# Single-row fetches on ScalarE's queue beside SP's, in a graph network's edge loop that gathers with GpSimd

## The chip, the cores and the metric

The kernel runs on one core of a Trainium2 chip. The metric is the device time of one execution in microseconds (us); the time given for a kernel is the median of several runs. A core has TensorE (PE), VectorE (DVE), ScalarE (ACT), GpSimd (POOL) and SyncE (SP). Each has its own instruction queue and works through it in order. DMAs are issued from the queues of SP, ACT and POOL, and 16 DMA engines carry them out.

## What is computed

One layer of a graph network over 12,500 nodes and 200,000 edges, with 64 features for each node and edge, and after it a layer norm. Cut to what matters, with `ssp(v) = softplus(v) - log 2`:

```
nodes    = x[edges]                      # (src, dst) of each edge: 2 x 64 features
gates    = (ssp(edge_state @ We1 + be1) @ We2 + be2) * soft_cutoff(distance)
h        = ssp(nodes @ Wn1 + bn1) @ Wn2 + bn2
sums     = zeros_like(x).at[dst].add(h * gates)
x_new    = x + ssp(sums @ Ws1 + bs1) @ Ws2 + bs2
out      = layernorm(x + x_new)
```

The edges are sorted by `dst`; `src` is random. So the rows `x[src]` have to be gathered one by one, while the `dst` side of 256 neighbouring edges falls into a window of 42 nodes.

## The kernel before

**Groups and steps.** The edges are cut into 391 groups of 512 (`GE`), each in K = 4 slots of 128 edges. A loop (line 573) goes over steps i from -3 to 388; each step does a different stage of several groups, so that the stages of one group are spread over several steps. The order on each engine is the order of the program text (`manual_schedule`). A step before `ends` = 380 does this:

- `load(i + 5)` (line 218): three DMAs on SP, the edge features eT of the group (128 KB) and two tables of 42 rows, wns. Each waits until an earlier group's scatter is over.
- `fetch(i)` (line 203): single rows of x on SP, see below.
- `gather(i + 14)` (line 189): one indirect DMA on POOL for each slot, 128 rows of x by the indices of `src`, into a tile xg; there are 18 such tiles.
- `layer2_edge(i - 1)` (line 282) on PE. Its first matmul (line 285) takes the step's waits in one place: through `behind` it waits for the gather and the one-hot matrix of group i + 3, the copy xT of group i + 1 and the load of group i + 1. The matmuls that need these come later in the step and need not stop for them.
- `layer1_edge(i + 1)` and `layer1_node(i + 1)` (lines 254 and 260) into a PSUM tile z, and the scatter of group i - 3 (line 312), whose result lies in the same tile.
- `exps(i + 1)` and `logs(i + 1)` (lines 271 and 274) on ACT: the exponential and the logarithm of the softplus.
- `transposes(i + 3)` (line 243) on PE, which read the gathered rows, and `xcopy(i + 3)` (line 248) on ACT, which takes them from PSUM to SBUF.
- `layer2_node(i - 1)` (line 295) on PE, and then `hcut`, `message`, `window`, `softplus(i + 1)` and `onehot(i + 5)` on DVE (lines 304, 308, 329, 279 and 234). `window` first loads two register values (line 320).

Whenever enough groups are complete, a block of 512 nodes is finished beside the loop: its parts (25 blocks in all) are put into steps by `BLOCK_STEPS`. From step 380 on the order changes, so that the pipeline runs empty: the transposes come ahead of the matmuls of layer 1, and `layer2(g)` calls `layer2_edge` as before, so that it waits for the gather of group g + 4 (line 287) although its step transposes an earlier group or none. The last group and the last node block follow behind the loop.

**Single rows.** In twelve groups (36, 68, ..., 388, every 32nd: `slots_by_rows`, line 101) POOL gathers only three of the four slots. The 128 rows of the last slot, K - 1, are fetched by SP: in each of the steps 0 to 383, `fetch` loads four indices into SP's registers (line 210) and issues four DMAs of one row of 256 bytes (line 214) into a tile xr, of which there are two. So a slot is complete after 32 steps, and its group is transposed two steps later. For such a group DVE also copies the slot's one-hot columns from xg to xr (line 236). Each of these DMAs is noted among the group's gathers, for which line 285 waits.

Of the kernel before, what the change touches and what calls it, by code (L numbers as in the profile page):

```python
# [42 lines left out]
F32 = mybir.dt.float32  # L43
# [8 lines left out]
SP = mybir.EngineType.SP  # L52
# [4 lines left out]
P = 128  # L57
D = 64
# [3 lines left out]
DW = D + W  # L62
PIECES = 3
NB = 512
K = 4
# [10 lines left out]
ROWS = 4  # L76
# [23 lines left out]

def slots_by_rows(NG):

    return [g for g in range(P // ROWS + 4, NG - 2, P // ROWS)]


@with_exitstack
def gnn_resnorm_kernel(ctx: ExitStack, tc: tile.TileContext, a: dict, out: bass.AP, E: int):
    nc = tc.nc
    x = a["x"]
    N = x.shape[0]  # L110
    NG = a["eT"].shape[1]
# [10 lines left out]
    loads = ctx.enter_context(tc.tile_pool(name="loads", bufs=LOADS + 2))  # L122
# [26 lines left out]
    packed, at = {}, 0  # L149
# [18 lines left out]
    xgs, xrs, eTs = {}, {}, {}  # L168
    made = {}

    def note(key, ins):
        made.setdefault(key, []).append(ins)
        return ins

    def behind(ins, *keys):

        for key in keys:
            for other in made.get(key, []):
                tc.add_manual_dep(ins.ins, other.ins.name,
                                  mybir.DependencyInfo(mybir.DependencyClass.Sync, mybir.DependencyReason.DATA),  # L180
                                  reason="one place of a step takes its waits")

    by_rows = slots_by_rows(NG)
    rows_i = const.tile([len(by_rows), P], I32, name="rows_i")

    def padding(g, k):
        return g * GE + k % 2 * HE + k // 2 * P >= E

    def gather(g, after=False):

        xg = loads.tile([P, K, P], F32, name="xg", bufs=AHEAD + BEHIND)
        xgs[g] = xg
        if after:
            nc.vector.memset(xg[:, 0, :1], 0.0)
        for k in range(K - (g in by_rows)):
            if padding(g, k):
                nc.vector.memset(xg[:, k, :D], 0.0)
                continue
            note(("gather", g), nc.gpsimd.indirect_dma_start(  # L199
                out=xg[:, k, :D], out_offset=None, in_=x,  # L200
                in_offset=bass.IndirectOffsetOnAxis(ap=src_i[:, g, k : k + 1], axis=0)))

    def fetch(i):

        n, r = divmod(i * ROWS, P)
        if i < 0 or n >= len(by_rows):
            return
        if r == 0:
            xrs[by_rows[n]] = loads.tile([P, P], F32, name="xr", bufs=2)
        _, at = nc.values_load_multi_w_load_instructions(  # L210
            rows_i[n : n + 1, r : r + ROWS], engines=[SP], min_val=0, max_val=N - 1,
            skip_runtime_bounds_check_because="src holds rows of x")
        for j, v in enumerate(at):
            note(("gather", by_rows[n]), nc.sync.dma_start(xrs[by_rows[n]][r + j : r + j + 1, :D], x[bass.ds(v, 1), :]))  # L214

    bases = {}

    def load(g):
# [13 lines left out]

    def onehot(g):
        last = nc.vector.tensor_tensor(xgs[g][:, :, D:DW], iota, rel[:, g, :].to_broadcast([P, K, W]), OP.is_equal)  # L234
        if g in by_rows:
            last = nc.vector.tensor_copy(xrs[g][:, D:DW], xgs[g][:, K - 1, D:DW])
        note(("onehot", g), last)

    def transposes(g):
        tx = tx_tile()[:DW].rearrange("f (k e) -> f k e", k=K)  # L240
        for k in range(K):
            row = xrs[g][:, :DW] if g in by_rows and k == K - 1 else xgs[g][:, k, :DW]
            nc.tensor.transpose(tx[:, k, :], row, ident)  # L243
        xTs[g] = tx

# [33 lines left out]
        nc.vector.scalar_tensor_tensor(ss[g].rearrange("p i t e -> p (i t e)")[:, part], us[g][:, part], BIG,  # L279
                                       z_of(g)[:, part], OP.min, OP.max)  # L280

    def layer2_edge(g):
        gh = gh_tile()
        v = gh.rearrange("p (i t h d) -> p i t h d", i=2, t=2, h=2)
        first = nc.tensor.matmul(gh, ones3[:, :P], row3.rearrange("q i k d -> q (i k d)"), start=True, stop=False,  # L285
                                 skip_group_check=True)
        behind(first, ("gather", g + 4), ("onehot", g + 4), ("xcopy", g + 2), ("load", g + 2))
        for t in range(2):
            nc.tensor.matmul(v[:, 0, t], ss[g][:, 0, t, :], we2, start=False, stop=False, skip_group_check=True)  # L289
        ghs[g] = gh.rearrange("p (i k d) -> p i k d", i=2, k=K)  # L290
# [128 lines left out]
    with tc.manual_schedule():  # L419
# [4 lines left out]
        with tc.tile_pool(name="prep", bufs=1) as prep:  # L424
# [67 lines left out]
            for i, w in enumerate((we2[:D, 0, :], wn2)):  # L492
                n = w.shape[0]
# [16 lines left out]
            rows = prep.tile([PIECES, 4, D], BF16, name="rows")  # L510
# [6 lines left out]
            for i in range(PARTS):  # L517
# [19 lines left out]
                if i == 2:  # L537
# [5 lines left out]
                    for t in range(2):  # L543
                        r = rel[:, :, 2 * t : 2 * t + 2]
# [3 lines left out]
        with tc.tile_pool(name="finish", bufs=1) as finish:  # L548
            blocks = list(zip(node_blocks(N), block_steps(N, NG)))
            last = NG - 1  # L550
            ends = last - CATCH_UP
            second, third, ahead = {}, {}, {}
# [12 lines left out]
            def at(f, g, *more):  # L565
                if 0 <= g < NG:
                    f(g, *more)
# [5 lines left out]
            for i in range(-3, last - 1):  # L573
                now = parts.pop(i, [])
                early = [part for part in now if part.tensor]
                at(load, i + LOADS)
                fetch(i)
                if i >= 0:
                    at(gather, i + AHEAD, i < BEHIND)
                if i < ends:  # L580
                    for g in second[i]:
                        layer2_edge(g)
                    if i >= -1:
                        zs[i + 1] = z_tile()
                        layer1_edge(i + 1)
                        for part in early:
                            part.tensor(tx_tile())
                    if i >= -1:
                        layer1_node(i + 1)
                    for n, g in enumerate(third[i]):  # L590
                        scatter(g, zs[i + 1][:, 1, HE + 2 * W * n : HE + 2 * W * (n + 1)])
                    at(exps, i + 1)
                    at(logs, i + 1)
                    for g in ahead[i]:
                        transposes(g)
                        xcopy(g)
                    for g in second[i]:
                        layer2_node(g)
                    for g in second[i]:
                        hcut(g)  # L600
                        message(g)
                    for g in third[i]:
                        window(g)
                    for part in early:
                        part.others()
                    at(softplus, i + 1)
                else:
                    for g in ahead[i]:
# [73 lines left out]
            for part in begun:  # L682
# [4 lines left out]
                         skip_runtime_bounds_check_because="a comparison's result")  # L687
    with tc.If(far > 0), tc.tile_pool(name="outside", bufs=1) as o:
# [7 lines left out]
        with tc.For_i(0, NG, 1) as g:  # L696
# [38 lines left out]
            v = gh.rearrange("p (i k d) -> p i k d", i=2, k=K)  # L735
# [27 lines left out]
def layouts(inputs):  # L763
# [3 lines left out]
    x = np.asarray(inputs["x"])  # L767
# [3 lines left out]
    N, E = x.shape[0], src.shape[0]  # L771
# [10 lines left out]

    out = {"x": np.ascontiguousarray(x)}
    out["src_l"] = lanes(src, 0)
    out["rows"] = np.ascontiguousarray(out["src_l"].reshape(P, NG, K)[:, slots_by_rows(NG), K - 1].T)
    out["dst_l"] = lanes(dst, dst[-1])
    out["dist_l"] = lanes(dist, 1e6)
    out["dst_h"] = np.ascontiguousarray(padded(dst, NR * P * HE, dst[-1]).reshape(NR, P, HE).transpose(1, 0, 2))
# [42 lines left out]
```

## Time and profile before

| | |
|---|---|
| time, median of 3 runs | 2012.66 us (2009.44 to 2016.36) |
| profiled execution: its own time | 2006.9 us |
| profiled execution: span, first to last instruction | 2005.1 us |
| mean granted TensorE clock | 0.971 of full speed |
| PE busy | 1853.3 us, 92% |
| POOL busy | 1477.0 us, 74%, 1555 instructions |
| DVE busy | 1079.6 us, 54% |
| ACT busy | 921.0 us, 46% |
| row DMAs on SP (line 214) | 1536, 228 ns each on the queue (median) |

In the profile, L199 means line 199 of the kernel. An entry of a group ends with the busy time in us, the mean duration in ns, the idle time of the engine just ahead of these instructions, and after an arrow what ended most of that idle time. PEld is TensorE's weight load, which lies beside its matmuls; SPq is SP's queue, where issuing a DMA isn't counted as busy. Where an instruction waits for several things, the profile names the one that came last by its own account; if the one named had long been over, it was another. The granted clock is 1.00 when TensorE runs at its full clock.

### The profile page before, as it was taken

How to read it: one execution, taken by the hardware profiler on the slowest of the kernel's cores; microseconds unless marked ns; L12 is line 12 of the kernel's file. 1: busy time of each engine (PE TensorE's matmuls, PEld its weight loads, DVE VectorE, ACT ScalarE, POOL GpSimd, SP SyncE). 2: the span in 40 equal slices, each digit the busy share in tenths (PEclk: the TensorE clock that was granted, in tenths of full speed). 3: DMA queues.
4: the chain of work that ended last, by engine and by line, in shares of the span. 5: the costliest groups of instructions: out<-in, count | busy, mean ns of one | idle time of the engine just before them, and what ended most of it. 6: DMA issues, size and time to landing. Idle time of an engine off the chain costs nothing.

```text
span 2005.1 us, 41203 instructions
## 1 busy us (share of the span) xinstructions
PE 1853.3 (92%) x11373; PEld 1539.3 (77%) x11373; DVE 1079.6 (54%) x2744; ACT 921.0 (46%) x1318; POOL 1477.0 (74%) x1555
## 2 busy tenths in 40 slices
PE   5899999989999988998999899999999999999997
PEld 4788888877777777777777777778777777777875
DVE  4455555544554554545555555545555555555654
ACT  1355555544444444444444444445444444444543
POOL 6777777777777777777777777777777777777770
PEclk9999999999999999999999999989999999998997
DMA  8422222222222222222222222222222222222320
GB/s 238 131 69 70 70 71 69 71 65 62 66 65 65 62 65 65 65 65 67 62 68 65 65 68 64 68 61 71 70 66 68 67 68 68 68 70 64 74 63 12
DMA packets 170980, 143.09 MB, mean 71 GB/s; under 512 B 46475, under 2 KB 142915, under 8 KB 170746
## 3 DMA queue, kind: packets, MB, share of 16 engines
q1 hardware_dynamic: 119746, 87.95, 15.1%
q0 software_dynamic: 49632, 50.92, 13.4%
q10 hardware_dynamic: 1368, 1.51, 0.3%
q8 instruction: 97, 1.59, 0.3%
q14 instruction: 137, 1.12, 0.2%
HBM read 130.57 MB, written 9.63 MB: 70 GB/s over the span
## 4 chain that ended last, share of the span: by engine, by line
PE 81%; DMA 6%; ACT 5%; issue 3%; DVE 2%; SPq 2%; POOL 0%; DVEq 0%; ACTq 0%
PE z L260 17%; PE gh L289 12%; PE z L254 12%; PE gh L295 12%; PE z L312 8%; PE gh L285 6%; PE tx L243 6%; PE z L252 4%; DMA eT<-in_eT 4%; ACT u L271 2%; ACT u L274 2%; PE z L522 2%; PE tx L348 1%; PE tx L379 1%; SPq L214 1%
## 5 line engine op out<-in xcount | busy, mean ns | idle before, releaser
L199 POOL DMA_INDIRECT xg<-in_x,src_i x1551 | 1476.8, 952 | 480.4 <-issue 343.9
L271 ACT ACTIVATE u<-z 128x768 f32<-128x768 f32 x392 | 317.4, 810 | 981.4 <-PE z L312 953.6
L304 DVE TENSOR_TENSOR h<-gh,cut 128x256 f32<-128x256 f32 x391 | 166.0, 425 | 707.7 <-PE gh L295 702.7
L260 PE MATMUL z<-xT,wns 106*128 106x256 f32 x1564 | 422.2, 393 | 0.0
L295 PE MATMUL gh<-consts,s 128*128 128x64 f32 x3128 | 396.4, 270 | 0.0
L295 PEld LDWEIGHTS gh<-consts,s 128*128 128x128 f32 x3128 | 384.9, 194 | 0.0
L279 DVE SCALAR_TENSOR_TENSOR s<-u,z 128x768 f32<-128x768 f32 x392 | 372.7, 951 | 20.0 <-ACT u L274 6.8
L274 ACT ACTIVATE u<-u,one 128x768 f32<-128x768 f32 x392 | 365.8, 933 | 12.7
L260 PEld LDWEIGHTS z<-xT,wns 106*128 106x128 f32 x1564 | 306.8, 198 | 46.6 <-ACT xT L248 0.7
L289 PE MATMUL gh<-consts,s 128*128 128x128 f32 x1564 | 281.0, 302 | 0.0
L254 PE MATMUL z<-eT,consts 128*128 128x256 f32 x782 | 280.3, 441 | 0.0
L289 PEld LDWEIGHTS gh<-consts,s 128*128 128x128 f32 x1564 | 205.8, 191 | 91.5 <-issue 91.0
L312 PEld LDWEIGHTS z<-xg,msg 128*128 128x128 f32 x1512 | 237.4, 198 | 22.5
L285 PE MATMUL gh<-row,ones 3*128 3x512 bf16 x391 | 148.7, 380 | 105.6 <-DMA eT<-in_eT 28.2
L243 PE MATMUL tx<-consts,xg 128*106 128x128 f32 x1552 | 239.6, 278 | 4.1 <-DVE xg L234 2.7
L248 ACT COPY xT<-tx 106x512 f32<-106x512 f32 x391 | 221.4, 566 | 15.8 <-PE tx L243 15.8
L312 PE MATMUL z<-xg,msg 128*128 128x84 f32 x1512 | 223.5, 271 | 0.0
L329 DVE TENSOR_TENSOR sums<-sums,z 64x42 f32 x756 | 148.6, 197 | 131.2 <-ACT xT L248 108.1
L243 PEld LDWEIGHTS tx<-consts,xg 128*106 128x106 f32 x1552 | 185.3, 144 | 5.0 <-DVE xg L234 3.0
L308 DVE TENSOR_TENSOR msg<-gh,h 128x256 f32<-128x256 f32 x391 | 165.8, 424 | 13.4
L254 PEld LDWEIGHTS z<-eT,consts 128*128 128x128 f32 x782 | 118.4, 191 | 47.9 <-issue 2.2
L285 PEld LDWEIGHTS <-ones 3*128 3x128 bf16 x391 | 35.4, 91 | 142.3 <-ACT u L274 58.1
(101 smaller groups left out, 682.6 us busy)
## 6 DMA issues: line engine op xcount, KB each, us to landing
eT<-in_eT SPq DMA_DIRECT2D x391, 128.0 KB
xg<-in_x,src_i POOLq DMA_INDIRECT x1551
xr<-in_x SPq DMA_DIRECT2D x1536, 0.2 KB
wns<-table SPq DMA_DIRECT2D x782, 21.0 KB
table<-tb SPq DMA_DIRECT2D x14, 448.0 KB
sums<-in_xT SPq DMA_DIRECT2D x7, 455.0 KB
y<-in_x SPq DMA_DIRECT2D x24, 128.0 KB
out<-y SPq DMA_DIRECT2D x24, 128.0 KB
```

The lines of the kernel that those rows point to most:

```text
L199: note(("gather", g), nc.gpsimd.indirect_dma_start(out=xg[:, k, :D], out_offset=None, in_=x, in_offset=bass.IndirectOffsetOnAxis(ap=src_i[ ...
L243: nc.tensor.transpose(tx[:, k, :], row, ident)
L248: note(("xcopy", g), nc.scalar.copy(xT, xTs[g]))
L254: nc.tensor.matmul(zs[g][:, 0, :HE], we1.rearrange("a h d -> a (h d)"), eTs[g], start=False, stop=True, skip_group_check=True)
L260: nc.tensor.matmul(zn, wns[:, g % REST, h, :], xTs[g][:, h], start=True, stop=True, skip_group_check=True)
L271: nc.scalar.activation(us[g][:, part], z_of(g)[:, part], AF.Exp)
L274: nc.scalar.activation(us[g][:, part], us[g][:, part], AF.Ln, bias=one)
L279: nc.vector.scalar_tensor_tensor(ss[g].rearrange("p i t e -> p (i t e)")[:, part], us[g][:, part], BIG, z_of(g)[:, part], OP.min, OP.max)
L285: first = nc.tensor.matmul(gh, ones3[:, :P], row3.rearrange("q i k d -> q (i k d)"), start=True, stop=False, skip_group_check=True)
L289: nc.tensor.matmul(v[:, 0, t], ss[g][:, 0, t, :], we2, start=False, stop=False, skip_group_check=True)
L295: nc.tensor.matmul(ghs[g][:, 1, 2 * t + h, :], ss[g][:, 1 + h, t, :], wn2, start=False, stop=h == 1 and t == 1, skip_group_check=True)
L312: ins = nc.tensor.matmul(sc, msgs[g][:, 2 * t : 2 * t + 2, :].rearrange("p h f -> p (h f)"), xgs[g][:, 2 * t : 2 * t + 2, D:DW], start=t = ...
```

## The change

The number of slots fetched by single rows is doubled. In each of the twelve groups slot K - 2 is now fetched in this way too, so that POOL gathers two of the four slots there. SP goes on fetching slot K - 1. ACT's queue fetches slot K - 2: in each step one load of four indices into ACT's registers and two row DMAs stand between the exponential and the logarithm, and two more between the logarithm and the copy xT. The new tiles have a name for each of the two slots, two buffers each. The calls on ACT stand in the branch for steps before 380; the rows of steps 380 to 383, the last 16 of slot K - 2 of group 388, are therefore not fetched, and ACT issues 380 x 4 = 1520 of them.

The second part concerns the waits of line 285. In steps before 380 they are put together from the groups which the step itself transposes (`ahead[i]`, which is i + 3 there), and are the same as before. From step 380 on `layer2_edge` is called without any, so that each instruction waits for its own inputs alone.

```
 def slots_by_rows(NG):
-    return [g for g in range(P // ROWS + 4, NG - 2, P // ROWS)]
+    return [(g, k) for k in (K - 1, K - 2) for g in range(P // ROWS + 4, NG - 2, P // ROWS)]
...
+    half_of = {nc.sync: 0, nc.scalar: len(by_rows) // 2}
...
-        for k in range(K - (g in by_rows)):
+        for k in range(K):
+            if (g, k) in by_rows:
+                continue
...
-    def fetch(i):
+    def fetch(i, engine, first=0, count=ROWS):
-        n, r = divmod(i * ROWS, P)
-        if i < 0 or n >= len(by_rows):
+        n, r = divmod(i * ROWS + first, P)
+        if i < 0 or n >= len(by_rows) // 2:
             return
+        n += half_of[engine]
         if r == 0:
-            xrs[by_rows[n]] = loads.tile([P, P], F32, name="xr", bufs=2)
-        _, at = nc.values_load_multi_w_load_instructions(
-            rows_i[n : n + 1, r : r + ROWS], engines=[SP], min_val=0, max_val=N - 1,
-            skip_runtime_bounds_check_because="src holds rows of x")
-        for j, v in enumerate(at):
-            note(("gather", by_rows[n]), nc.sync.dma_start(xrs[by_rows[n]][r + j : r + j + 1, :D], x[bass.ds(v, 1), :]))
+            xrs[by_rows[n]] = loads.tile([P, P], F32, name=f"xr{by_rows[n][1]}", bufs=2)
+        if first == 0:
+            _, row_at[engine] = nc.values_load_multi_w_load_instructions(
+                rows_i[n : n + 1, r : r + ROWS], engines=[engine.engine], min_val=0, max_val=N - 1,
+                skip_runtime_bounds_check_because="src holds rows of x")
+        for j in range(count):
+            note(("gather", by_rows[n][0]), engine.dma_start(xrs[by_rows[n]][r + j : r + j + 1, :D],
+                                                             x[bass.ds(row_at[engine][first + j], 1), :]))
...
     def onehot(g):
...
-        if g in by_rows:
-            last = nc.vector.tensor_copy(xrs[g][:, D:DW], xgs[g][:, K - 1, D:DW])
+        for k in range(K):
+            if (g, k) in by_rows:
+                last = nc.vector.tensor_copy(xrs[g, k][:, D:DW], xgs[g][:, k, D:DW])
...
-    def layer2_edge(g):
+    def layer2_edge(g, *needs):
...
-        behind(first, ("gather", g + 4), ("onehot", g + 4), ("xcopy", g + 2), ("load", g + 2))
+        behind(first, *needs)
...
-                fetch(i)
+                fetch(i, nc.sync)
...
                 if i < ends:
+                    needs = [("xcopy", i + 1), ("load", i + 1)]
+                    needs += [(name, g) for g in ahead[i] for name in ("gather", "onehot")]
                     for g in second[i]:
-                        layer2_edge(g)
+                        layer2_edge(g, *needs)
...
                     at(exps, i + 1)
+                    fetch(i, nc.scalar, 0, ROWS // 2)
                     at(logs, i + 1)
+                    fetch(i, nc.scalar, ROWS // 2, ROWS // 2)
                     for g in ahead[i]:
                         transposes(g)
                         xcopy(g)
```

More of the change, by code (lines that the diff above doesn't have):

```diff
@@ L201, in gather @@
                 in_offset=bass.IndirectOffsetOnAxis(ap=src_i[:, g, k : k + 1], axis=0)))
-    def fetch(i):
-        n, r = divmod(i * ROWS, P)
-        if i < 0 or n >= len(by_rows):
+    def fetch(i, engine, first=0, count=ROWS):
+        n, r = divmod(i * ROWS + first, P)
+        if i < 0 or n >= len(by_rows) // 2:
             return
+        n += half_of[engine]
         if r == 0:
-            xrs[by_rows[n]] = loads.tile([P, P], F32, name="xr", bufs=2)
-        _, at = nc.values_load_multi_w_load_instructions(
-            rows_i[n : n + 1, r : r + ROWS], engines=[SP], min_val=0, max_val=N - 1,
-            skip_runtime_bounds_check_because="src holds rows of x")
-        for j, v in enumerate(at):
-            note(("gather", by_rows[n]), nc.sync.dma_start(xrs[by_rows[n]][r + j : r + j + 1, :D], x[bass.ds(v, 1), :]))
+            xrs[by_rows[n]] = loads.tile([P, P], F32, name=f"xr{by_rows[n][1]}", bufs=2)
[6 more added lines that the diff above has]
+                                                             x[bass.ds(row_at[engine][first + j], 1), :]))
+    row_at = {}
     bases = {}
@@ L241, in transposes @@
         for k in range(K):
-            row = xrs[g][:, :DW] if g in by_rows and k == K - 1 else xgs[g][:, k, :DW]
+            row = xrs[g, k][:, :DW] if (g, k) in by_rows else xgs[g][:, k, :DW]
             nc.tensor.transpose(tx[:, k, :], row, ident)
@@ L784, in layouts @@
     out["src_l"] = lanes(src, 0)
-    out["rows"] = np.ascontiguousarray(out["src_l"].reshape(P, NG, K)[:, slots_by_rows(NG), K - 1].T)
+    out["rows"] = np.ascontiguousarray(out["src_l"].reshape(P, NG, K)[(slice(None), *zip(*slots_by_rows(NG)))].T)
     out["dst_l"] = lanes(dst, dst[-1])
```

## The prediction, made before the changed kernel had run

> **What bounds the kernel now.** I read the page's busy times and groups first, then busy time by stretches of 50 us, then the timeline of two steps in the middle, then the waits.
>
> The groups, page:
>
> ```profile
> L199 POOL DMA_INDIRECT xg<-in_x,src_i x1551 | 1476.8, 952 | 480.4 <-issue 343.9
> L271 ACT ACTIVATE u<-z 128x768 f32<-128x768 f32 x392 | 317.4, 810 | 981.4 <-PE z L312 953.6
> ...
> L274 ACT ACTIVATE u<-u,one 128x768 f32<-128x768 f32 x392 | 365.8, 933 | 12.7
> ```
>
> PE is busy 92% of the span and POOL only 74%, yet POOL's busy and idle time add up to 1476.8 + 480.4 = 1957 us, which is all of the time until its last gather (start 1956.7). The idle time comes in pieces of 0.3 us, one between every two gathers, so it is part of a gather's price. The stretches show what this means (columns: PE, PEld, DVE, ACT, POOL busy; granted clock; DMA share; GB/s):
>
> ```profile
> 150.00:200.00 50.00, 50.00 (x320) 41.77 (x320) 28.25 (x71) 25.71 (x35) 37.81 (x41) 1.00 0.29 70
> ...
> 700.00:750.00 50.00, 43.70 (x281) 36.45 (x280) 26.44 (x69) 23.32 (x35) 37.81 (x41) 1.00 0.27 66
> ...
> 1000.00:1050.00 50.00, 46.07 (x285) 38.22 (x284) 27.25 (x71) 22.93 (x34) 37.94 (x40) 0.97 0.28 68
> ```
>
> POOL does 40 to 41 gathers in every stretch, early or late. PE has no idle time until about 390 us and idles in every stretch afterwards. PE starts with a lead of 14 gathered groups, uses it up, and then runs at POOL's pace. The timeline, all engines, shows it in one step:
>
> ```profile
> 999.70 0.95 POOL L199 DMA_INDIRECT xg<-in_x,src_i  x1 [0.30 <-DMA xg<-in_x,src_i]
> ...
> 1000.38 1.50 SPq L214 DMA_DIRECT2D xr<-in_x  x4
> ...
> 1000.95 0.94 POOL L199 DMA_INDIRECT xg<-in_x,src_i  x1 [0.30 <-issue]
> ...
> 1002.13 0.81 ACT L271 ACTIVATE u<-z 128x768 f32<-128x768 f32 x1 [2.10 <-PE z L312]
> 1002.20 0.95 POOL L199 DMA_INDIRECT xg<-in_x,src_i  x1 [0.30 <-PE z L312]
> ...
> 1003.87 0.37 PE L285 MATMUL gh<-row,ones 3*128 3x512 bf16 x1 [0.50 <-DMA eT<-in_eT]
> ```
>
> The gathers stand 1.25 us apart. L285 is the place where a step takes its waits. The wait is named eT, but eT is issued steps ahead of its use. Counting gathers (four a group, less the slots not gathered), the one that began at 1000.95 is the last of group 198, which this step (195) needs; its last packet is done about 2.15 us after the start (median of all gathers in the trace), and 0.8 us later L285 goes. From step 72 on, nearly every step that isn't catching up after a half-clock stretch has this same 0.8 us. While PE still had its lead, L285 came every 4.35 us; a step with a node block's matmuls takes 5.2. POOL's period is 127 gathers per 32 steps, 127 x 1.25 / 32 = 4.96 us. So POOL sets the pace up to step 379 (L285 at 1922.01), the last main step. The other 83 us, to 2005.1, are PE's own catch-up steps and the last node block.
>
> **Fewer gathers.** Each of twelve groups loses one more gather: 1551 becomes 1539. Eleven of the twelve groups come before group 382, the last that step 379 needs. 11 x 1.25 = 13.75 us on the path; the twelfth leaves POOL's end alone. PE can follow: the new period is 126 x 1.25 / 32 = 4.92 us, against a mean step without waits of 4.65 us (steps 72 to 379, node blocks and half-clock stretches included). Replaying the trace step by step (a step starts when the step before plus its own unwaited time is over and its gather has landed) with eleven gathers less gives 13.75 us at step 379.
>
> The Trainium skill speaks against this: "DMA: Bandwidth & Descriptors", section "Issuing engines are not separate DMA queues", says that DMAs from any queue share 16 engines, and spreading them saves only issue time, usually small. Were transfers the bound, the gain would be 0. Here the DMA engines are busy 0.27 to 0.30 of a stretch and POOL's issue alone fills the period; the saved issue time is the 1.25 us of the row, so I take 13.75.
>
> **ScalarE's new work.** In steps 0 to 379 it gets one register load and four row fetches, in two pairs. SP does the same now: the load (L210) has a median of 0.56 us, four rows take 1.50 us from first start to last end, about 0.41 each with their register operations. Together 0.56 + 4 x 0.41 = 2.2 us a step. Is it beside the activations or between them? The nearest row is VectorE's register load for the window (L320), in the waits:
>
> ```profile
> DVE sums L329 <- ACT xT L248: 108.1, 332, 0.7
> ```
>
> In the trace's records that load begins 13 ns after the message product (L308, at 1013.99) has begun, runs beside it, and leaves 0.32 us of idle before L329; the ScalarE copy named there ends 0.2 us too early to be the reason. So a queue's own instruction runs beside the engine's instruction ahead of it, and what is longer than that shows. For ScalarE: load and two rows take about 1.43 us from the start of exp (0.81 us), so the logarithm starts 0.6 us later; the second pair (0.82 us) fits beside the logarithm (0.93 us). The PSUM copy xT is thus also 0.6 us later. The lower bound is 0, were all of it issued in the 2.43 us (median) for which ScalarE idles before exp; the upper is 2.2 us, if nothing overlaps. I take 0.6.
>
> Behind it wait: the xT copy (read 5 us or more later by L260), VectorE's window, which starts 0.2 us after that copy, and then the softplus (L279), up to 0.4 us later. The softplus ends 2.7 us (median; 1.65 in the early PE-bound steps, 1.3 at the 5th percentile) ahead of L285 two steps on, which reads it. So it costs 0 on the path; without that cover it would be 0.4 us a step.
>
> **Queues and semaphores.** Each DMA of SP waits in the records for the semaphore that it raises, and eight of these go round; ScalarE's DMAs of the preamble draw on the same eight. With 11 instead of 7 a step, SP's rows of one step would wait for ScalarE's of the step before, and ScalarE's for SP's loads of its own step. One round of that takes two steps: row lands 1.23 us after issue, then SP's rest and loads 1.8, then eT 2.14 and wns 1.78 us to land: about 6.4 us where two steps have 9.8. SP's lead falls from three steps to about one, but its loads are due four steps later. Cost 0; a gain is excluded, since PE never waits for SP now. The last row of a slot comes some 3.5 us ahead of L285. The twelve extra VectorE copies (0.05 to 0.2 us) hide in VectorE's 46% idle.
>
> **The last steps.** Steps 380 to 388 drop waits for groups that they don't use. In the trace they had landed, and the only idle time there is 0.35 us (L285 at 1939.16, for VectorE). Between 0 and 0.35; I take 0, since L243 at 1960.11 waits 1.35 us for VectorE anyway.
>
> **Sum.** The profiled execution took 2006.9 us (span 2005.1): 2006.9 - 13.75 = 1993.2. The median of the three runs is 2012.66, 5.8 higher; PE's half-clock stretches in the tail (1961, 1975, 1995 us) are what such runs can differ by. 2012.66 - 13.75 = 1998.9, so 1999.0.
>
> **Rivals.**
> - Slower: ScalarE's queue does the loads and fetches strictly between its activations. Then logarithm plus copy come 2.2 us later and the softplus about 2.07. The loop is L285, 3.16 us to exp, 3.9 us from there through logarithm, window and softplus to L285 two steps on: 7.05 plus the delay in two steps of 4.92, less 0.87 with a node block. In the replay a softplus delay of up to 1.5 us leaves 13.5 or more, 2.0 leaves 4.4, 2.2 loses 19: it decides from about 2 us. At 2.07 it is a loss of about 4, 2017. For it: the logarithm follows exp at once now (12.7 us idle in all), so nothing is known of ScalarE's queue with work between. Against: VectorE's row.
> - Part of the gain: the delay lies between 1.5 and 2 us, or the shared semaphores hold ScalarE up when transfers are late (the 99th percentile of eT is 3.7 us). About 6 us left, 2007.
> - No gain: PE is the bound (92% busy), or its clock falls as its load rises; 2012.7. Against: the 4.35 us steps, and the first half-clock stretch comes at 473 us, after the waits began, none in the 290 us of full load.
>
> **Chances.** Hidden as worked out 0.77 (1993 to 2005, by the runs' spread and the tail's clock), part 0.08, no gain 0.04, slower 0.11. The range 1992 to 2009 takes in the first and second. A measurement can tell 0.3%, 6.0 us: faster (under 2006.6) 0.80, the same 0.09, slower 0.11.
>
> **What would show it.** L199 x1539, still 1.25 us apart, the last near 1942; PE's idle before L285 about 92 us instead of 105.6; idle before L274 some 0.6 x 380 = 230 us instead of 12.7; idle before L271 less by as much; L279 without new waits; span near 1991. Idle before L279 or L285 named for ScalarE would show the slower rival; gathers further than 1.25 us apart, or a tail longer than 83 us, would break the sum.

## The result, and the profile after

The median is 1994.42 us (1991.83 to 1998.7), against 2012.66 before. The ratio is 0.9934, 95% interval [0.991, 0.9957]: 13.3 us of 2012.66 by the ratio, with 8.7 to 18.1 as the interval's ends. The two medians lie 18.2 us apart, just beyond that interval. The profiled execution took 1994.42 us with a span of 1992.6, 12.5 less than the span before. The median lies 4.6 us under the predicted 1999.0.

The groups that answer to those shown of before, and two more (page of the changed kernel; busy time, mean ns, idle time ahead of them and what ended it). L202, L279, L282, L287 and L293 are the gather, the exponential, the logarithm, the softplus and PE's first waits, which were L199, L271, L274, L279 and L285.

```profile
L202 POOL DMA_INDIRECT xg<-in_x,src_i x1539 | 1463.6, 951 | 477.8 <-issue 336.7
L279 ACT ACTIVATE u<-z 128x768 f32<-128x768 f32 x392 | 317.4, 810 | 659.1 <-PE z L320 625.3
...
L282 ACT ACTIVATE u<-u,one 128x768 f32<-128x768 f32 x392 | 365.9, 933 | 304.4 <-DMA xr<-in_x 294.6
...
L287 DVE SCALAR_TENSOR_TENSOR s<-u,z 128x768 f32<-128x768 f32 x392 | 372.8, 951 | 24.3 <-ACT u L282 7.2
...
L293 PE MATMUL gh<-row,ones 3*128 3x512 bf16 x391 | 148.9, 381 | 103.1 <-DMA xr<-in_x 47.8
```

POOL has twelve gathers less and the same price for each: busy and idle together are 1941.4 us for 1539, against 1957.2 for 1551. The last gather starts at 1940.9, 15.8 us earlier. The logarithm's idle time rose from 12.7 to 304.4 us, and the idle time ahead of the exponential fell by 322.3: ScalarE's new work moved a wait and made none. The softplus' idle time hardly moved (20.0 before).

The stretches (columns as in the prediction), of which the second and third have the same times as there:

```profile
200.00:250.00 50.00, 46.85 (x260) 38.95 (x260) 23.16 (x60) 21.05 (x29) 37.83 (x40) 0.86 0.27 64
700.00:750.00 50.00, 45.61 (x283) 37.86 (x282) 25.83 (x66) 23.03 (x33) 37.80 (x41) 0.97 0.27 66
1000.00:1050.00 50.00, 45.42 (x293) 37.94 (x292) 26.76 (x69) 23.03 (x33) 37.93 (x40) 1.00 0.30 72
```

POOL still does 40 to 41 gathers in 50 us. The DMA engines are no busier. New is the clock of 0.86 between 200 and 250 us, where PE had run at full clock without idle time; it is taken up below.

One step in the middle, ScalarE's and VectorE's part of the timeline:

```profile
1001.68 0.81 ACT L279 ACTIVATE u<-z 128x768 f32<-128x768 f32 x1 [2.11 <-PE z L320]
...
1002.38 1.17 ACTq L219 DMA_DIRECT2D xr<-in_x  x2
...
1003.60 0.94 ACT L282 ACTIVATE u<-u,one 128x768 f32<-128x768 f32 x1 [1.11 <-DMA xr<-in_x]
1003.75 0.61 ACTq L219 DMA_DIRECT2D xr<-in_x  x2
...
1004.15 0.41 DVE L337 TENSOR_TENSOR sums<-sums,z 64x42 f32 x2 [0.31 <-issue]
...
1004.44 0.56 ACT L256 COPY xT<-tx 106x512 f32<-106x512 f32 x1
...
1004.91 0.95 DVE L287 SCALAR_TENSOR_TENSOR s<-u,z 128x768 f32<-128x768 f32 x1
```

The first two rows are issued while the exponential runs and hold up the logarithm, here by 1.11 us (the gap's median over all steps is 0.78, before 0.03); the other two lie beside the logarithm. VectorE's window (L337) begins before the copy, so it doesn't wait for it, and the softplus follows 0.37 us after the logarithm's end, where the median before was 1.14. The 0.75 us that the logarithm lost came out of that gap.

### The profile page after: what moved, and what is told of

Same layout as the page of the kernel before. It is cut to its first block, busy times and chain, and to the rows that moved or that the text cites. A ratio compares the mean times of both kernels' runs of the same rounds, so it can differ in the third digit from the quotient of the medians.

```text
span 1992.6 us, 46151 instructions
## 1 busy us (share of the span) xinstructions
PE 1843.2 (92%) x11373; PEld 1531.6 (77%) x11373; DVE 1082.5 (54%) x2756; ACT 925.0 (46%) x1318; POOL 1463.8 (73%) x1543
## 3 DMA queue, kind: packets, MB, share of 16 engines
q14 instruction: 176, 1.43, 0.2%
## 4 chain that ended last, share of the span: by engine, by line
PE 73%; SPq 8%; DMA 7%; issue 5%; DVE 2%; ACT 2%; ACTq 1%; POOL 1%; DVEq 0%; POOLq 0%
PE z L268 15%; PE gh L303 11%; PE gh L297 11%; PE z L262 10%; PE z L320 7%; PE tx L251 6%; PE gh L293 6%; DMA xr<-in_x 6%; PE z L260 3%; SPq L235 3%; SPq L219 2%; SPq L215 2%; PE z L530 2%; ACT u L279 2%; DVE h L312 1%
## 5 line engine op out<-in xcount | busy, mean ns | idle before, releaser
L202 POOL DMA_INDIRECT xg<-in_x,src_i x1539 | 1463.6, 951 | 477.8 <-issue 336.7
L279 ACT ACTIVATE u<-z 128x768 f32<-128x768 f32 x392 | 317.4, 810 | 659.1 <-PE z L320 625.3
L282 ACT ACTIVATE u<-u,one 128x768 f32<-128x768 f32 x392 | 365.9, 933 | 304.4 <-DMA xr<-in_x 294.6
L268 PE MATMUL z<-xT,wns 106*128 106x256 f32 x1564 | 415.9, 389 | 0.0
L287 DVE SCALAR_TENSOR_TENSOR s<-u,z 128x768 f32<-128x768 f32 x392 | 372.8, 951 | 24.3 <-ACT u L282 7.2
L268 PEld LDWEIGHTS z<-xT,wns 106*128 106x128 f32 x1564 | 302.1, 195 | 44.8 <-ACT xT L256 0.7
L293 PE MATMUL gh<-row,ones 3*128 3x512 bf16 x391 | 148.9, 381 | 103.1 <-DMA xr<-in_x 47.8
L337 DVE TENSOR_TENSOR sums<-sums,z 64x42 f32 x756 | 148.5, 196 | 129.9 <-issue 116.7
L293 PEld LDWEIGHTS <-ones 3*128 3x128 bf16 x391 | 35.5, 91 | 140.2 <-issue 122.1
```

Of the source, the lines that this page charges most:

```text
L202: note(("gather", g), nc.gpsimd.indirect_dma_start(out=xg[:, k, :D], out_offset=None, in_=x, in_offset=bass.IndirectOffsetOnAxis(ap=src_i[ ...
L268: nc.tensor.matmul(zn, wns[:, g % REST, h, :], xTs[g][:, h], start=True, stop=True, skip_group_check=True)
L279: nc.scalar.activation(us[g][:, part], z_of(g)[:, part], AF.Exp)
L282: nc.scalar.activation(us[g][:, part], us[g][:, part], AF.Ln, bias=one)
```

## The experiments

The kernels of one group ran on one chip together with the kernel before; every ratio is to that one. The first four came together (before: 2011.57 us), to cut the change into its parts.

**The dropped waits alone.** The kernel before, with the changed `layer2_edge` and its calls:

```
-    def layer2_edge(g):
+    def layer2_edge(g, *needs):
-        behind(first, ("gather", g + 4), ("onehot", g + 4), ("xcopy", g + 2), ("load", g + 2))
+        behind(first, *needs)
```

> The kernel before, with the waits of the last steps dropped alone. Theory (the gain is eleven gathers less on GpSimd's queue): no change, ratio 1.000, since the waits of steps 380 to 388 had ended before they were asked for; at most 0.35 us. Rival (the dropped waits give part of the gain): some us faster, and less than 83 us from L285 of step 379 to the end.

Measured: 2009.92 us, ratio 0.9992 [0.9977, 1.0008]. The second part of the change is worth nothing that can be measured.

**The rows alone.** The changed kernel, with the old waits in `layer2_edge`:

```
-        behind(first, *needs)
+        behind(first, ("gather", g + 4), ("onehot", g + 4), ("xcopy", g + 2), ("load", g + 2))
```

> The changed kernel, with the old waits in every step. Theory: the whole gain stays, about 13.8 us, ratio 0.993, L285's counterpart of step 379 near 1907 us. Rival (the waits give part): some us slower than the changed kernel.

Measured: 1989.9 us, 0.991 [0.9886, 0.9933]. The whole gain is in the rows.

**ScalarE's work without fewer gathers.** The changed kernel; POOL gathers the second slot too, and the fetched rows of it aren't used:

```
-            if (g, k) in by_rows:
+            if (g, k) in by_rows and k == K - 1:
```

(in `gather`, `onehot` and `transposes` alike).

> The changed kernel, but GpSimd gathers slot K - 2 of the twelve groups too, and it is read from there; what ScalarE fetches is not read. So all the added work is there and nothing is taken off GpSimd. Theory: 1551 gathers again 1.25 us apart, time as before, ratio 1.000, while the logarithm still starts 0.8 us later. Rival (ScalarE's issuing costs time on the path, and the gain of the change is net of it): slower than before, by up to 0.4 us a step, 150 us.

Measured: 2008.28 us, 0.9988 [0.9973, 1.0002].

**Fewer gathers without ScalarE's work.** The kernel before, with one more slot left out of POOL's gathers:

```
+        if g in by_rows:
+            nc.vector.memset(xg[:, K - 2, :D], 0.0)
-        for k in range(K - (g in by_rows)):
+        for k in range(K - 2 * (g in by_rows)):
```

> The kernel before, but GpSimd leaves slot K - 2 of the twelve groups out and nobody fetches it: these 12 x 128 edges are worked on with zeros as their source rows. Theory: the same as the changed kernel, ratio 0.993, 13.8 us, since the issuing is hidden. Rival (the issuing costs): faster than the changed kernel by what the issuing costs.

Measured: 1992.47 us, 0.9916 [0.9893, 0.9939]. The same two groups of the page, first of the kernel with ScalarE's work alone, then of the one with fewer gathers alone:

```profile
L202 POOL DMA_INDIRECT xg<-in_x,src_i x1551 | 1475.9, 952 | 482.6 <-issue 316.7
...
L282 ACT ACTIVATE u<-u,one 128x768 f32<-128x768 f32 x392 | 365.9, 933 | 304.1 <-DMA xr<-in_x 295.2
```

```profile
L201 POOL DMA_INDIRECT xg<-in_x,src_i x1539 | 1464.8, 952 | 477.5 <-issue 330.4
...
L276 ACT ACTIVATE u<-u,one 128x768 f32<-128x768 f32 x392 | 365.8, 933 | 12.7
```

The time goes with the count of gathers, not with the logarithm's wait. At step 379 (L285 there, and the same matmul in the others) the five traces stand at 1922.0 (before), 1920.6 (waits alone), 1923.2 (ScalarE's work alone), 1908.7 (fewer gathers alone) and 1907.2 (changed). The price of the rows and their gain are separate and add up; traces with the same number of gathers differ by up to 2.6 us there.

The next three came together as well (before: 2009.32 us). They ask where the room on ScalarE's queue ends.

**Rows behind the copy.** Does it matter that the logarithm waits?

```
-                    fetch(i, nc.scalar, 0, ROWS // 2)
                     at(logs, i + 1)
-                    fetch(i, nc.scalar, ROWS // 2, ROWS // 2)
                     for g in ahead[i]:
                         transposes(g)
                         xcopy(g)
+                    fetch(i, nc.scalar)
```

> The changed kernel with ScalarE's load and all four rows behind the copy xT, in the time in which ScalarE waits for the next step's z. The logarithm follows the exponential at once again (0.03 us). Theory (the 0.8 us ahead of the logarithm are hidden, and GpSimd sets the pace): same time as the changed kernel, 0.993. Rival (that gap costs something): faster than the changed kernel by it.

Measured: 1991.29 us, 0.9926 [0.9906, 0.9946]. In its page the logarithm again follows the exponential at once, and the wait stands where it was before:

```profile
L279 ACT ACTIVATE u<-z 128x768 f32<-128x768 f32 x392 | 316.9, 808 | 884.1 <-PE z L320 779.3
...
L282 ACT ACTIVATE u<-u,one 128x768 f32<-128x768 f32 x392 | 365.7, 933 | 12.7
```

291.7 us less of waiting at the logarithm bring no time: the changed kernel's 0.78 us a step is hidden, as forecast.

**Both slots on SP.** The same DMAs, all eight rows a step from one queue:

```
-                fetch(i, nc.sync)
+                fetch(i, nc.sync)
+                fetch(i, nc.sync, 1)
```

(`fetch` takes the slot; ScalarE's calls are gone.)

> The changed kernel, but SP fetches both slots: 1539 gathers and no work on ScalarE. Theory (issue time of a queue is what is scarce): SP's step is then 0.36 + 0.06 for eT, 0.85 for wns, 0.25 for their register load, 2 x 0.6 for two register loads and 8 x 0.41 for rows, about 6.0 us, more than GpSimd's 4.92, so SP sets the pace: near 384 x 1.08 = 415 us slower than the kernel before less its lead, about 2400 us. Rival (SP's time is hidden behind waits that it has anyway): as the changed kernel, 0.993.

Measured: 2643.73 us, 1.3164 [1.3127, 1.32]. SP's queue in the timeline of this kernel:

```profile
1497.01 4.14 SPq L219 DMA_DIRECT2D xr<-in_x  x8
1501.26 0.37 SPq L228 DMA_DIRECT2D eT<-in_eT  x1
1501.81 0.85 SPq L235 DMA_DIRECT2D wns<-table  x2
1503.46 3.79 SPq L219 DMA_DIRECT2D xr<-in_x  x8
```

SP issues almost without a gap and needs 6.45 us for this step; the mean between steps 72 and 379 is 6.5. The mechanism is as expected, the size was 0.45 us a step too small: in these two steps the eight rows with the register load between them take 4.14 and 3.79 us (3.9 by my sum), and the rest takes 2.3 to 2.8 (2.1). Here the issue time of one queue is the pace of the whole kernel, with the same transfers.

**Four more rows on ScalarE, read by nobody.** This was meant to measure the prediction's slower rival: a softplus some 1.3 us later.

```
                     fetch(i, nc.scalar, 0, ROWS // 2)
+                    extra(i, 4)
                     at(logs, i + 1)
```

where `extra` issues `nc.scalar.dma_start` four times, for the indices that are in ScalarE's registers, into a tile of its own.

> The changed kernel with four more row fetches a step on ScalarE between the exponential and the logarithm (the same four indices, into a tile that nothing reads). At 0.41 us each the logarithm starts 0.78 + 1.64 = 2.4 us after the exponential's end, and the softplus 1.3 us later than before. By the prediction's replay (it decides from about 2 us of delay of the softplus) nothing is lost: as the changed kernel, 0.993. Rival A (ScalarE's own queue decides: 2.32 us of activations, 0.12 of node blocks and 2.4 of wait are 4.86 us a step beside GpSimd's 4.92): the catching up after half-clock stretches is lost, some 10 to 60 us slower than the changed kernel. Rival B (the eight shared semaphores decide): SP trails ScalarE further, and TensorE idles at the twelve groups with fetched rows and before loads.

Measured: 2663.07 us (2636.74 to 2725.5), 1.32 [1.3135, 1.3266]. No expectation was near: some 650 us more than the kernel before.

**A third slot by rows.** Slot K - 3 too, its four rows behind the copy xT, one load of eight indices, and ScalarE's calls also in the steps from 380 on:

```
-    return [(g, k) for k in (K - 1, K - 2) for g in range(P // ROWS + 4, NG - 2, P // ROWS)]
+    return [(g, k) for k in (K - 1, K - 2, K - 3) for g in range(P // ROWS + 4, NG - 2, P // ROWS)]
...
                         xcopy(g)
+                    fetch(i, nc.scalar, 2)
```

(`fetch` takes the slot here, and loads eight indices for ScalarE's two.)

> ScalarE fetches a third slot (K - 3) of the twelve groups too: two rows behind the exponential, two behind the logarithm, four behind the copy xT, one load of eight indices; its calls stand in the last steps as well, so all rows are fetched. 1527 gathers, 125 in 32 steps, 4.88 us a step against TensorE's 4.65. Theory: 22 gathers of 1.25 us come off the path, 27.5 us, ratio 0.986, and the logarithm still starts about 0.8 us late. Rival (the shared semaphores, now with 15 DMAs a step, make SP trail ScalarE so far that rows or loads come late): TensorE idles before the step's first matmul without a gather being late, and part of the gain or all of it is lost.

Measured: 2868.48 us, 1.43 [1.4254, 1.4345]. Missed again, and by more, although the longest new work stands behind the copy, where four rows had cost nothing. ScalarE's waits in this kernel (what waits, for what: us in total, times, longest; L281 is the exponential, L284 the logarithm):

```profile
ACT u L284 <- DMA xr<-in_x: 583.9, 381, 5.1
ACT u L281 <- DMA xr<-in_x: 513.8, 228, 7.9
```

Waits of up to 7.9 us aren't the time that an issue takes: ScalarE's row DMAs themselves stand still.

The timeline of the kernel with four more rows shows what stops them there. One step (L332 is the scatter, L294 the logarithm, L299 the softplus, L268 the copy xT, L305 PE's first waits):

```profile
1506.28 0.57 PE L332 MATMUL z<-xg,msg 128*128 128x84 f32 x4
1506.29 0.94 ACT L294 ACTIVATE u<-u,one 128x768 f32<-128x768 f32 x1 [2.73 <-DMA xd<-in_x]
1506.44 2.87 ACTq L219 DMA_DIRECT2D xr<-in_x  x2
...
1506.89 0.36 SPq L240 DMA_DIRECT2D eT<-in_eT  x1
...
1507.26 0.95 DVE L299 SCALAR_TENSOR_TENSOR s<-u,z 128x768 f32<-128x768 f32 x1 [2.12 <-ACT u L294]
...
1509.35 0.59 ACT L268 COPY xT<-tx 106x512 f32<-106x512 f32 x1 [2.13 <-DMA eT<-in_eT]
...
1510.00 0.41 PE L305 MATMUL gh<-row,ones 3*128 3x512 bf16 x1 [1.86 <-ACT xT L268]
```

Two row DMAs take 2.87 us on ScalarE's queue, and the copy behind them is released by eT, a load that it doesn't read. In the records, eT lands at 1509.07 and the second row goes at 1509.09. Eight semaphores are shared by the DMAs of SP and ScalarE, and in the records each DMA waits until the one before it on its semaphore has landed. So ScalarE's row waits for a load of SP's. ScalarE is in step 218 here, and the load is that of step 222. SP issues it only once the scatter that last used its buffers has ended (1506.85; issue at 1506.89), and that scatter is of PE's step at hand, 219. The circle is closed: scatter, eT's issue, 2.2 us to land, ScalarE's row, the copy, PE's next step. From the first waits of this step (1503.73) to those of the next it takes 6.27 us; the mean step between 72 and 379 is 6.59, against 4.99 before. In the same records of the kernel the softplus' end is within 0.4 us ahead of L305 in 31% of the steps, and the copy's in 30%: both of ScalarE's results are late, by the same waits. The waits are not all of the loss. In the profiled spans PE's idle time ahead of its first waits grows by 220 us (105.6 to 326.0), but its busy time by 382 (1853.3 to 2235.4): with idle time in every step it runs at half clock for 944 us of the span, where it was 116.

Which DMA stands before which comes with the program: it is the same in the traces of the changed kernel, of the rows alone and of ScalarE's work alone, and differs between other kernels that look alike. By the order of the DMAs on each semaphore, ScalarE's rows of step i stand behind SP's loads of step i - 1 or i in the changed kernel; of i + 3 or i + 4 with four more rows, and with a third slot. With the rows behind the copy they stand behind loads of i to i + 3, and few of them behind i + 3 (47 of some 1200); those go 2.2 us or more after the scatter, and the logarithm and the copy of the step stand ahead of them. For the third slot the order is all that was read, not a step like the one above.

That is a reading of one kernel's records. Four more kernels test it, on a third chip. There the kernel before itself took 2708.46 us (2691.95 to 2726.46), so only the ratios and differences within this group are used, and the times expected in us can't be compared. No trace of the kernel before is there. In the four traces the last gather that a step needs starts 65 to 76 us (median) ahead of its first waits, so GpSimd isn't the bound on that chip. What differs is SP's queue. Its register moves ahead of the rows, in the changed kernel and in the last of the four (minimum, median and longest in ns):

```profile
L219 SPq MOVE xr<-in_x x1536: 29/29/38, 86.0 to 1930.0; - x192
```

```profile
L219 SPq MOVE xr<-in_x x1536: 2/29/1397, 100.7 to 2533.0; - x192
```

All four have such stalls, and none of the other ten traces has. In the last of the four, SP's queue loses 2.5 us a step (0.1 in the changed kernel) to instructions and gaps that are longer than usual with no semaphore to wait for, and PE idles 4.2 to 8.6 us ahead of eleven of the twelve groups with fetched rows. So SP's queue is likely what made that chip slow; that is argued, not tested. These records are disturbed themselves: some 70% of the semaphore updates are missing (the second of the four has 6917, the changed kernel's trace 23718 for as many DMAs), so the names of waits there tell little.

**Register loads in place of rows.** This was meant to keep ScalarE as long as with four more rows, without a DMA more (three loads of four unused values behind the first pair):

```
                     fetch(i, nc.scalar, 0, ROWS // 2)
+                    extra(i, 3)
                     at(logs, i + 1)
```

> The changed kernel with three more register loads on ScalarE (0.55 us each) between the exponential and the logarithm, no DMA more than the changed kernel has. In the built program this puts ScalarE's rows of step i behind SP's loads of step i + 3 on the shared semaphores, as in the kernel with four more rows. Theory (closed loop): slower by hundreds of us although no DMA was added. Rival (only the number of DMAs or ScalarE's own 2.4 us matter): 2.32 + 0.12 + 2.4 us fit into 4.92, so at most some 60 us slower than the changed kernel.

Measured: 2848.84 us, 1.0493 [1.0427, 1.056]. The trace shows another kernel than the one that was meant (L215 is the register load, L228 the line of the three):

```profile
L215 ACTq TENSOR_LOAD <-rows_i x380: 483/489/748, 92.5 to 2747.6; - x190
```

```profile
L228 ACTq EVENT_SEMAPHORE  x1140: 3/17/17, 94.1 to 2749.3; - x190
```

The three loads, whose values nothing uses, aren't there: ScalarE does one load a step, as in the changed kernel, and three semaphore instructions of 17 ns. So this is no test of ScalarE's time. It is one of the order: ScalarE has the changed kernel's loads and rows and hardly more, but the rows stand behind loads of step i + 3 (a few of i + 4). It is 261 us slower than the changed kernel with all its rows (2587.93 us, below), which has them behind loads of step i - 1 or i.

**The same, with the order tied.** SP's load of eT for group g also waits for the exponential of group g - 5 (`LOADS` is 5), so that the program is built with the loads behind it; the rows then stand behind loads of step i + 1:

```
-        behind(note(("load", g), nc.sync.dma_start(eTs[g], a["eT"][:, g, :])), old)
+        behind(note(("load", g), nc.sync.dma_start(eTs[g], a["eT"][:, g, :])), old, ("exps", g - LOADS))
...
-        nc.scalar.activation(us[g][:, part], z_of(g)[:, part], AF.Exp)
+        note(("exps", g), nc.scalar.activation(us[g][:, part], z_of(g)[:, part], AF.Exp))
```

> As the one before, with the load of group g also behind the exponential of group g - 5, which puts ScalarE's rows behind SP's loads of the next step at most, and only those behind the logarithm. Theory: without the loop ScalarE's own delay is what is left; the logarithm starts 2.4 us after the exponential and the softplus 1.3 us later than before, which the prediction's replay calls free: 0.993, at most 60 us more if ScalarE's 4.86 us a step can't catch up after half-clock stretches. Rival (ScalarE's delay alone makes the loss): as the one before.

Measured: 2572.05 us, 0.9497 [0.9455, 0.954]. Here too ScalarE has 380 register loads: the three aren't in this kernel either.

**Four more rows, tied** by the same line:

> The kernel with four more rows (2663 us), and nothing else than that the load of group g also waits for the exponential of group g - 5, so that SP can't run three steps ahead. Theory now (a closed loop through the eight shared semaphores: ScalarE's row waits for the landing of an eT that SP issues only when TensorE has done the scatter of the same step; 2.1 us in every step between scatter and logarithm): the loop is broken, the loads have landed when the next step's rows ask, and most of the 650 us come back, below 2150 us. Rival (ScalarE's own time for ten queue instructions a step is too long): no change, about 2660 us.

Measured: 2623.01 us, 0.9689 [0.9637, 0.9741].

**The changed kernel with its last sixteen rows.** ScalarE's two calls also in the branch from step 380 on, where the change leaves rows 112 to 127 of one slot unfetched:

```
                 else:
+                    fetch(i, nc.scalar, 0, ROWS // 2)
...
+                    fetch(i, nc.scalar, ROWS // 2, ROWS // 2)
```

> The changed kernel with ScalarE's calls in steps 380 to 383 too, so that all 1536 rows of the second slot are fetched. Theory: those steps wait for no gather, sixteen rows more cost nothing: as the changed kernel, 0.993. Rival (the last steps are bound by TensorE and have no cover): up to 4 x 0.8 = 3 us slower.

Measured: 2587.93 us, 0.9545 [0.9502, 0.9587]. The changed kernel itself didn't run on this chip, so what the sixteen rows cost is not shown.

The page's rows of the two kernels whose three loads fell away, untied and then tied (L291 is the logarithm, L302 PE's first waits, L265 the copy):

```profile
L291 ACT ACTIVATE u<-u,one 128x768 f32<-128x768 f32 x392 | 365.9, 933 | 960.9 <-DMA xr<-in_x 411.6
...
L302 PE MATMUL gh<-row,ones 3*128 3x512 bf16 x391 | 173.9, 445 | 419.3 <-ACT xT L265 217.2
```

```profile
L291 ACT ACTIVATE u<-u,one 128x768 f32<-128x768 f32 x392 | 365.9, 933 | 557.4 <-DMA xr<-in_x 500.1
...
L302 PE MATMUL gh<-row,ones 3*128 3x512 bf16 x391 | 164.0, 419 | 330.4 <-ACT xT L265 151.0
```

Both do the same work on ScalarE. One added wait makes the kernel 277 us faster (2848.84 to 2572.05): the order, not the length of the work, had cost that much. In the profiled spans, 281 us apart, PE's idle time ahead of L302 is 89 us less and its busy time 176 (2323.3 to 2146.9), at half clock for 762 us instead of 1193.

What the length of ScalarE's work costs is hardly tested. With the order tied, four more rows take 35 us more than the changed kernel with all its rows (2623.01 against 2587.93), on a chip where a step takes 6.4 us in both, so that ScalarE had some 1.5 us more room in it than at GpSimd's 4.92. The 1.32 of four more rows can't be set beside the 0.9689 with the tie, since the chips differ; untied it wasn't run on the third chip, nor tied on the others.

## Why the prediction was right, and where not

**POOL sets the pace, eleven gathers: right.** 13.75 us were predicted at step 379, 14.8 measured (1922.0 to 1907.2). Eleven times 1.25 is in it; the rest is the mean distance of gathers, 1.2542 us against 1.2551 before, some 1.3 us over 1500 gathers, which is no more than traces of the same number of gathers differ by. Fewer gathers alone give 0.9916. The rule of the Trainium skill that I weighed ("DMA: Bandwidth & Descriptors", section "Issuing engines are not separate DMA queues": the queues share the DMA engines, and spreading saves only issue time, usually small) holds in its first half: the DMA engines were busy 0.25 to 0.31 of a 50 us stretch before and after. What it calls usually small was here all that counts, 13.3 us gained by taking issue from POOL and 1.3164 times the time with all rows on SP.

**ScalarE's queue runs beside its activations: right in kind.** The register load begins 6 ns after the exponential has begun (VectorE's row had shown 13). The logarithm was 0.78 us late instead of 0.6: the load takes 0.49 us, but the first row's DMA instruction takes 0.45 where later ones take 0.22, which the sum of 1.43 us for a load and two rows left out. Cost 0 on the path, as forecast: ScalarE's work alone gives 0.9988, rows behind the copy the same gain.

**The softplus up to 0.4 us later: mis-sized, it is 0.** It rested on a window that starts 0.2 us after the copy. The window doesn't wait for the copy (1004.15 and 1004.44 in the step above). The softplus' cover ahead of the matmul that reads it stays 2.68 us (median).

**"Read 5 us or more later by L260": wrong place.** The copy is needed earlier, by the waits of L293 two steps on, with a median slack of some 3.4 us (2.5 at the 5th percentile). It was enough.

**"SP's lead falls from three steps to about one": it falls further, to none.** Before, SP issued its rows of a step 8.5 us (median) before PE's first waits of that step; after, 3.65 us behind them. That is 12 us, or 2.5 steps, from less than two. In the chain of waits of the changed kernel SP's queue has 8% of the span (before 2%):

```profile
PE 73%; SPq 8%; DMA 7%; issue 5%; DVE 2%; ACT 2%; ACTq 1%; POOL 1%; DVEq 0%; POOLq 0%
```

Cost 0 still, nearly: at eleven of the twelve groups with rows, L293 goes 1.6 to 4.2 us (median 3.1) after the issue of SP's last row, which the prediction had put at some 3.5; a row lands in 1.34. The first of them, in the timeline:

```profile
220.96 0.84 ACTq L219 DMA_DIRECT2D xr<-in_x  x2
...
221.80 1.50 SPq L219 DMA_DIRECT2D xr<-in_x  x4
...
222.00 0.61 ACTq L219 DMA_DIRECT2D xr<-in_x  x2
...
224.65 0.37 PE L293 MATMUL gh<-row,ones 3*128 3x512 bf16 x1 [3.15 <-DMA xg<-in_x,src_i]
```

Two of SP's rows (222.66 and 223.08) wait for semaphores that ScalarE's rows of 220.96 and 221.58 raise; the second lands at 224.31. PE idles 3.15 us, for these rows by the records and not for the gather that is named, and 13.65 us at half clock follow: the 0.86 in the first stretch. Both other kernels with ScalarE's rows at this place, rows alone and ScalarE's work alone, have the same stall (3.24 and 3.36 us); before and with fewer gathers alone there is none. PE still had its lead here and lost nothing at the end: in step 72, L293 is 10.7 us later than before, and at step 379 it is 14.8 us earlier. Only the luck of its place hid it; a group for which SP's rows come late was not in the prediction.

**The last steps at 0: right.** 0.9992 for the dropped waits alone.

**A tail of 83 us: 85.4.** From step 379's first waits to the end. PE's time at half clock in the tail is 33.1 us in the changed kernel and 23.5 before. Over seven kernels the tail goes with it: 79.1 us with 17.5 (rows behind the copy), 79.8 with 16.5 (rows alone), 82.9 with 23.5 (waits alone), 86.5 with 35.8 (fewer gathers alone), 87.2 with 36.9 (ScalarE's work alone). The two, 14.8 - 2.3, make the span's 12.5.

**"PE's idle before L285 about 92 us": wrong, it is 103.1** (before 105.6). The prediction took all of the gain out of PE's idle time and left PE's own work as it was. In this run PE is at half clock for 91 us of the span instead of 116, and is busy 10.1 us less (1853.3 to 1843.2); as GpSimd sets the pace, that becomes idle time.

**The slower rival fell; its point wasn't measured.** ScalarE's loads and rows don't stand strictly between its activations, by the 6 ns above. The point at which a later softplus was to decide, "from about 2 us", can't be read from four more rows: 1.3 us were expected there, but the logarithm followed the exponential by 3.1 us (median) instead of 2.4, by waits that the prediction's replay doesn't have. What cost most is which load of SP's a row stands behind: those of the step before or its own cost nothing, those of three or four steps on close a circle through PE's scatter. This is shown by one step's records of four more rows, and by 261 and 277 us between kernels with nearly the same work on another chip. The prediction had looked at the shared semaphores for SP's lead, and for ScalarE only as a rival worth part of the gain, when transfers are late; it had called ScalarE's side safe with loads "of its own step". That was so in this build, by the order it happened to get.

**Open.** What stalls SP's queue on the third chip, and what the change's 0.9545 there is made of, since GpSimd isn't the bound. What four more rows would cost on the first two chips with the order tied, and whether a third slot would then gain another 13 us; neither was tried.

## What to carry to other kernels

Where the issue on one queue sets the pace, count its instructions: taking some to another engine's queue gained their full price here, as long as they run beside that engine's work and the next thing it owes has slack. Before adding DMAs to a second queue, look in the records at what each of them waits for: here the DMAs that share completion semaphores ordered the queues against each other, and a small edit can turn a harmless order into a circle through the critical engine. When an experiment moves the time far more than its work can explain, compare that order first. And before an experiment's result is read, look in its trace whether the added instructions are there: of three register loads whose values nothing uses, none was.

## What the runs showed that I had not expected

- The order of SP's and ScalarE's DMAs on the semaphores that they share was worth some 10% (261 us to the changed kernel with all its rows, 277 to the tied one), with the DMA engines far from busy.
- The waits themselves were the smaller part of what four more rows cost: PE's idle time ahead of its first waits grew by 220 us, its busy time by 382, at half clock for 944 us of the span.
- The tail's length, 79 to 87 us with the same work, follows PE's half-clock time there (16.5 to 36.9 us), so two profiled spans can differ by some 8 us for that alone, more than half of the change's gain.
- The first row DMA after a register load takes 0.45 us on ScalarE's queue, the next 0.22.
